# A four-layer image model: where one normalisation runs, and in which order the neighbourhood layer's parts are written

## The chip, the cores and the metric

The kernel runs on one core of one Trainium2 chip. The metric is the device time of one execution in microseconds (us). The engines are TensorE (PE in the profile; PEld is its weight load), VectorE (DVE), ScalarE (ACT), GpSimd (POOL) and SyncE (SP), which issues the transfers. Each engine runs its own instructions in the order in which they were written, and waits where an operand is not there yet or where the place of a result is still in use.

## The reference, cut to what matters

The input is a batch of four images of 56 x 56 pixels with 128 channels. Four layers follow each other. The change touches the first, and one step of the second.

```python
# layer 0: neighbourhood attention (7 x 7 window, 4 heads of 32 channels), then an MLP
xn = layernorm(x);  q, k, v = split(xn @ w_qkv + b_qkv)
x = x + softmax(q . k_window + rpb) @ v_window @ w_proj + b_proj
x = x + gelu(layernorm(x) @ w_fc1 + b_fc1) @ w_fc2 + b_fc2
# layer 1: a gated complex recurrence of 16 steps, per pixel and channel, on g = group_norm(x)
forget = sigmoid(g @ Wf + bf + 2);  let_in = sigmoid(g @ Wi + bi)
delta  = softplus(g @ Wd + bd) * 0.1
h = forget * (A h) + delta * let_in * (B g)          # 16 times; A, B: 2-D Fourier transforms of 7 x 7 kernels
x = x + h
# layer 2: softmax attention over 3136 tokens, and a mixture of 8 experts (2 chosen)
# layer 3: attention by distance, and experts that choose their tokens
```

The sixteen steps are not run one by one. The kernel multiplies them out through powers of the 2 x 2 step, with some 40 elementwise operations for each piece of an image.

## The kernel before, in words

**Stripes and periods.** `neighbourhood_of_safe_scores` works layer 0 off in 28 stripes, seven for each image, of eight pixel rows (four tiles of 112 pixels) each. One turn of its main loop is a period: it writes the 25 parts of the table `PERIOD` once, in the table's order. Every part has a lag: ("scores", 1) in period i works on stripe i+1, ("mlp_out", -2) on stripe i-2. So up to five stripes are under way at a time. The engines TensorE, VectorE and ScalarE take the work in exactly this order (`manual_schedule`); nothing reorders it.

**The parts.** `norm_ahead`, `tokens`, `keys`, `queries` and `values` prepare a stripe. `scores` and `more_scores` form the scores of the first four and the last three blocks of eight columns, and ScalarE takes their exponentials (L663). `bands` and `more_bands` multiply by the relative bias on VectorE (L670). `start_sums`, `sums` and `more_sums` add up on TensorE, `quotient` divides on VectorE. `project` and `add_attention` end the attention. `second_norm` takes the statistics on VectorE (L750) and the roots in nine small operations on GpSimd (L891 to L899). `norm_mlp` then scales the four tiles into `xn` on GpSimd (L582), `mlp_tokens` turns them on TensorE (L207), and `mlp_hidden`, `mlp_out` and `add_mlp` follow. `exp_table` and `gelu_table` run a one-element function (L833), so that ScalarE loads a table early.

**PSUM.** Most results of TensorE pass through one pool of two banks (`ps1`), which are given out in turn: a matmul group waits until the last but one user of the pool has been read. The scores and the MLP's hidden layer share one place of four banks (`s`).

**The recurrence of image 0 within it.** Layer 1 of image 0 runs inside layer 0 of the later images. `Recurrence.plan` lays its steps into the periods: an entry (2, 17, "sums") of `WORK` is written in the second period after the unit's base, ahead of the part at place 17 of `PERIOD`. An image has seven units, and a unit's base lies two periods behind the one before, so that two units overlap. The Fourier transforms of the kernels (`WAVES_AT`) come first, one piece in each of eight periods, and each piece first fetches a table of waves from memory (L1066). `BEGIN` places the group norm between the two. The transforms' small constants are written at (1, 0).

**A unit's places.** All values of a unit lie in one tile, `parts`, and many share a place with a value that is dead by then (L1159 on). Of these the prediction speaks of two: `one_e`, which ScalarE writes in `delta` (L1212), lies where VectorE's `ab` is until `pair` has read it, and `xs`, which ScalarE fills in `turned` (L1218), lies where `pq` is until `result` and `result_sum` have read it.

**The forget gate.** `forget` forms a sigmoid as 0.5 tanh(z/2) + 0.5: two tanh on ScalarE (L1194), and the last step on GpSimd (L1205). It runs in all 28 units, 21 of them in the later layers of images 1 to 3.

Of the kernel before, what the change touches and what calls it, by code (L numbers as in the profile page):

```python
# [9 lines left out]
F32 = mybir.dt.float32  # L10
BF16 = mybir.dt.bfloat16
AF = mybir.ActivationFunctionType
ALU = mybir.AluOpType
# [4 lines left out]
B, H, W, C = 4, 56, 56, 128  # L18
TOK = H * W
P = 2 * W  # L20
NT = TOK // P
GT = 4
# [16 lines left out]
NQ = EC // ET  # L39

PERIOD = (
    ("scores", 1),
    ("more_sums", 0),
    ("norm_ahead", 3),
    ("mlp_tokens", -1),
    ("values", 1),
    ("statistics", 1),
    ("constants", 1),
    ("quotient", 0),
    ("more_scores", 1),  # L50
    ("tokens", 3),
    ("bands", 1),
    ("mlp_out", -2),
    ("project", 0),
    ("add_mlp", -2),
    ("gelu_table", -2),
    ("mlp_hidden", -1),
    ("add_attention", 0),
    ("second_norm", 0),
    ("start_sums", 1),  # L60
    ("keys", 3),
    ("exp_table", 1),
    ("norm_mlp", 0),
    ("sums", 1),
    ("more_bands", 1),
    ("queries", 3),
)

WORK = (
    (1, 12, "softplus"),  # L70
    (3, 24, "statistics"),
    (2, 25, "product_of_sums"),
    (1, 17, "sources"),
    (1, 20, "forget"),
    (3, 0, "pair"),
    (1, 6, "let_in"),
    (1, 14, "softplus_sum"),
    (3, 6, "result"),
    (1, 7, "delta"),
    (1, 11, "logarithm"),  # L80
    (2, 6, "source_gate"),
    (3, 7, "result_sum"),
    (2, 11, "fourths_trace"),
    (3, 17, "turned_back"),
    (3, 20, "added"),
    (2, 1, "source"),
    (2, 7, "fourths"),
    (2, 6, "traces"),
    (1, 12, "turned"),
    (2, 17, "sums"),  # L90
    (3, 2, "steps"),
    (2, 24, "sums_of_fourths"),
)

BEGIN = (
    (0, 14, "tokens"),
    (1, 25, "mean"),
    (2, 24, "normalise"),
    (2, 19, "root"),
    (2, 11, "squares"),  # L100
)

WAVES_AT = (
    (1, 11, "magnitudes"),
    (0, 12, "squared"),
    (1, 25, "scaled"),
    (0, 1, "products"),
)
UNITS = 9
KK = 128  # L110
# [365 lines left out]
def neighbourhood_of_safe_scores(env: Env, f, work):  # L476
# [17 lines left out]
    with ExitStack() as ctx:  # L494
        tc, nc, ins = env.tc, env.nc, env.ins
        cp = ctx.enter_context(tc.tile_pool(name="n_const", bufs=1))
        bp = ctx.enter_context(tc.tile_pool(name="n_big", bufs=1))
        sp = ctx.enter_context(tc.tile_pool(name="n_small", bufs=3))
        wp = ctx.enter_context(tc.tile_pool(name="n_work", bufs=2))
# [4 lines left out]
        bands = []  # L504
# [34 lines left out]
        held = [{} for _ in range(n)]  # L539
        statistics = [{} for _ in range(B)]  # L540

        def tiles_of(i):
            b, s = stripes[i]
            return env.x[b], slice(s * GT, (s + 1) * GT)
# [29 lines left out]
                    ahead(pending[0])  # L574
                    pending[0] += 1

        def normalised(i):
            x, tiles = tiles_of(i)
            rs, off = held[i]["norm"]
            xn = wp.tile([P, GT, C], F32, tag="xn", name="xn")  # L580
            for j in range(GT):
                nc.gpsimd.tensor_scalar(  # L582
                    xn[:, j, :], x[:, tiles.start + j, :], rs[:, j : j + 1],
                    off[:, j : j + 1], ALU.mult, ALU.add,
                )
            return xn

        def first_norm(i):
            held[i]["xn"] = normalised(i)

        def of_stripe(a, i):

# [242 lines left out]
        with tc.manual_schedule(  # L835
            engines={mybir.EngineType.PE, mybir.EngineType.DVE, mybir.EngineType.Activation}
        ):
            rs, off = f["roots"]
            for i in range(2):
                held[i]["norm"] = (a[:, i * GT : (i + 1) * GT] for a in (rs, off))  # L840
                first_norm(i)
            for i in range(2):
                tokens(i)
                if i == 0:
                    constants()
                keys(i)
                queries(i)
            ahead(2)
            parts = {
                "norm_ahead": first_norm,  # L850
                "norm_mlp": first_norm,
                "exp_table": lambda i: table(AF.Exp),
                "mlp_out": mlp_out,
                "add_mlp": add_mlp,
                "scores": lambda i: weights(i, 0),
                "more_sums": lambda i: add_blocks(i, 1),
                "quotient": quotient,
                "values": values,
                "bands": lambda i: banded(i, 0),
                "mlp_tokens": mlp_tokens,  # L860
                "tokens": tokens,
                "more_scores": lambda i: weights(i, 1),
                "keys": keys,
                "queries": queries,
                "constants": lambda i: late_constants() if i == 0 else None,
                "gelu_table": lambda i: table(AF.Gelu),
                "mlp_hidden": mlp_hidden,
                "project": project,
                "add_attention": add_attention,
                "second_norm": second_norm,  # L870
                "more_bands": lambda i: banded(i, 1),
                "start_sums": start_sums,
                "sums": lambda i: add_blocks(i, 0),
                "statistics": lambda i: ahead_to(i + NG + 3),
            }
            for i in range(-1, n + 2):
                for at, (name, lag) in enumerate(PERIOD):
                    run_all(plan.get((i, at), ()))
                    if 0 <= i + lag < n:
                        parts[name](i + lag)  # L880
                run_all(plan.get((i, len(PERIOD)), ()))

# [114 lines left out]
class Recurrence:  # L997
# [10 lines left out]
    def __init__(self, env, ctx, late):  # L1008

        self.env, self.is_late = env, late  # L1010
        nc = env.nc
        cp = ctx.enter_context(env.tc.tile_pool(name="s_const", bufs=1, side="right"))
        self.gates_w = cp.tile([128, 3, C], F32, tag="gates_w", name="gates_w")

        self.gates_b = cp.tile([128, 4, 2], F32, tag="gates_b", name="gates_b")
        self.late = cp.tile([128, 1], F32, tag="late", name="late")

        self.group = cp.tile([128, C], F32, tag="group", name="group")
        self.tiny = cp.tile([128, 1], F32, tag="tiny", name="tiny")
        nc.gpsimd.memset(self.tiny, 1e-8)  # L1020

        self.fa = cp.tile([128, 3, HALF], F32, tag="fa", name="fa")
        self.fb = cp.tile([128, 2, HALF], F32, tag="fb", name="fb")
        self.fa2 = self.fa[:, 2, :]
        self.taps = cp.tile([WAVES, 2, 2, C2], F32, tag="taps", name="taps")
        self.xT = cp.tile([128, TOK], F32, tag="xT", name="xT")

        self.parts = cp.tile([128, 21, UT * P], F32, tag="parts", name="parts")
        self.small = ctx.enter_context(env.tc.tile_pool(name="s_small", bufs=2, side="right"))
# [79 lines left out]
    def steps(self, b, psum):  # L1109


        env, nc, sides = self.env, self.env.nc, self.SIDES
        sp, x, xT = self.small, env.x[b], self.xT
        held = {}
# [43 lines left out]
        def unit(t0):  # L1158
# [42 lines left out]
            def forget():  # L1201

                f = v["forget"]
                gate(0, f, AF.Tanh, 0.5)
                nc.gpsimd.tensor_scalar(f, f, 0.5, 0.5, ALU.mult, ALU.add)  # L1205

            def delta():
                gate(2, v["delta"], AF.Identity)
# [187 lines left out]
    def plan(self, psum, start, statistics, root_of_all):  # L1396


        plan = {}

        def put(i, at, step):
            plan.setdefault((i, at), []).append(step)

        def put_all(table, i, steps):
            for period, at, name in table:
                put(i + period, at, steps[name])

        constants, parts = self.transforms(psum)
        put(1, 0, constants)
        for i, steps in enumerate(parts, 1):  # L1410
            put_all(WAVES_AT, i, dict(zip(("products", "squared", "magnitudes", "scaled"), steps)))
        tokens, mean, squares, root, normalise, units = self.steps(0, psum)
        put_all(BEGIN, start, {
            "tokens": lambda: run_all(tokens), "mean": mean, "squares": lambda: run_all(squares),
            "root": root, "normalise": lambda: run_all(normalise),
        })
        for u, unit in enumerate(units):
            unit["statistics"] = lambda u=u: statistics(tiles_of(u))
            if unit is units[-1]:
                unit["statistics"] = lambda u=u: (statistics(tiles_of(u)), root_of_all())  # L1420
            put_all(WORK, start + 2 + 2 * u, unit)
        return plan
# [1380 lines left out]
def run_all(pieces):  # L2803
    for piece in pieces:
        piece()
# [203 lines left out]
```

## Time and profile before

| what | value |
|---|---|
| median of three runs | 2571.6 us (2569.08 to 2573.55) |
| the profiled execution | 2573.55 us; its span 2571.7 us, 1.9 us lie around it |
| busy: PE, DVE, ACT, POOL | 2415.7, 1845.8, 1502.2, 309.5 us |
| layer 0 with the recurrence of image 0 | from about 18 us to 644 us of the span |
| PE busy and granted clock, 100 to 200 us | 100.0 of 100 us, 1.00 |
| PE busy and granted clock, 300 to 400 us | 87.7 of 100 us, 0.92 |

Times in the profile's rows count from the start of the span. In a row of the timeline the first number is the start and the second the time from the first to the last of the merged instructions; the bracket at the end is how long the engine had stood idle before it, and for whom. A table by stages gives for each stretch its length, and then for PE, PEld, DVE, ACT and POOL the busy time and the number of instructions, the granted TensorE clock (1.00 is full), the share of time in which DMA engines were busy, and GB/s. One place in the loop is easy to find in every period: the matmul at L732, which begins `project`.

### The profile page before, as it was taken

The page shows a single profiled execution, that of the slowest core. Times are in us where ns is not written, and L with a number is a line of the kernel's source. Part 1 is how long each engine was busy: PE and PEld are TensorE (multiplying, and loading weights), DVE is VectorE, ACT ScalarE, POOL GpSimd, SP SyncE. Part 2 cuts the span into 40 slices and gives each one's busy share as a digit, 9 for nine tenths or more (in the row PEclk, how much of TensorE's full clock was granted, in tenths as well). Part 3 has the DMA queues.
Part 4 walks back from the last instruction along what each step waited for, and adds up shares of the span by engine and source line. Part 5 has one row for each costly group of instructions (what it writes and reads, how often), then busy time and mean ns, then how long its engine had stood idle before and what let it go on. Part 6 is the DMA issues. An engine that isn't in the chain of part 4 may idle for free.

```text
span 2571.7 us, 39538 instructions
## 1 busy us (share of the span) xinstructions
PE 2415.7 (94%) x14685; PEld 1304.8 (51%) x14685; DVE 1845.8 (72%) x5062; ACT 1502.2 (58%) x3205; POOL 309.5 (12%) x612
## 2 busy tenths in 40 slices
PE   5999988988999999999999999999999999997795
PEld 3777666666554555545554444444444433442334
DVE  4566787775599786889868777753788666767563
ACT  3888765664666654676432456565545665754680
POOL 5445454433000000000000000000000000000000
PEclk9999998999999999999999999999999998998687
DMA  5000000000000000000000000000000000002266
GB/s 138 15 8 2 2 2 1 2 2 2 9 1 1 1 1 1 1 1 1 12 1 1 1 1 1 1 1 1 1 1 1 1 1 1 1 1 94 87 257 192
DMA packets 39919, 53.97 MB, mean 21 GB/s; under 512 B 4104, under 2 KB 35443, under 8 KB 35620
## 3 DMA queue, kind: packets, MB, share of 16 engines
q1 hardware_dynamic: 39716, 51.34, 6.2%
q8 instruction: 118, 1.93, 0.3%
q14 instruction: 85, 0.70, 0.1%
HBM read 44.78 MB, written 6.42 MB: 20 GB/s over the span
## 4 chain that ended last, share of the span: by engine, by line


## 5 line engine op out<-in xcount | busy, mean ns | idle before, releaser
L2027 ACT ACTIVATE e<-s_ps 128x448 f32<-128x448 f32 x688 | 368.9, 542 | 531.6 <-PE s_ps L2020 527.2
L2020 PE MATMUL s_ps<-zT,xnT 128*128 128x448 f32 (+1 forms) x1400 | 651.2, 555 | 0.6 <-ACT e L2027 0.6
L2103 PE MATMUL o_ps<-e,keep 128*128 128x448 f32 (+1 forms) x1376 | 646.8, 553 | 0.0
L2103 PEld LDWEIGHTS o_ps<-e,keep 128*128 128x128 f32 (+1 forms) x1376 | 241.3, 190 | 214.6 <-issue 213.6
L2020 PEld LDWEIGHTS s_ps<-zT,xnT 128*128 128x128 f32 (+1 forms) x1400 | 240.7, 189 | 213.0 <-issue 192.8
L1830 ACT ACTIVATE d_ps<-d_ps,half 128x448 f32<-128x448 f32 (+1 forms) x384 | 232.2, 606 | 118.0 <-PE d_ps L1818 115.8
L1824 DVE TENSOR_REDUCE found<-d_ps 128x1 f32<-128x448 f32 x316 | 190.7, 618 | 75.0 <-PE d_ps L1818 72.9
L1550 PE MATMUL y_ps<-experts,xnT 128*112 128x512 f32 x448 | 215.5, 603 | 2.0 <-ACT d_ps L1830 1.7
L207 PE MATMUL xT_ps<-ident,xn 112*128 112x112 f32 x672 | 129.9, 289 | 62.0 <-POOL xn L582 41.4
L1555 DVE TENSOR_TENSOR gated<-y_ps,gate 112x512 f32<-112x512 f32 x224 | 151.5, 686 | 37.8 <-PE y_ps L1550 35.4
L207 PEld LDWEIGHTS xT_ps<-ident,xn 112*128 112x128 f32 x672 | 82.3, 146 | 148.1 <-POOL xn L582 54.9
L1560 DVE TENSOR_TENSOR gated<-gated 112x512 f32<-112x512 f32 (+1 forms) x336 | 152.2, 461 | 3.0
L1818 PE MATMUL d_ps<-q_near,k_near 32*128 32x448 bf16 (+1 forms) x700 | 138.2, 373 | 9.8 <-ACT d_ps L1830 4.0
L1550 PEld LDWEIGHTS y_ps<-experts,xnT 128*112 128x112 f32 x448 | 76.2, 178 | 97.6 <-issue 60.4
L1818 PEld LDWEIGHTS <-k_near 32*128 32x128 bf16 (+1 forms) x700 | 33.4, 92 | 168.1 <-issue 155.1
L582 POOL TENSOR_SCALAR xn<-x,rs,off 112x128 f32<-112x128 f32 x216 | 116.5, 552 | 3.2
L766 ACT ACTIVATE h<-h_ps,b_fc 128x448 f32<-128x448 f32 x112 | 61.7, 633 | 79.1 <-PE h_ps L761 79.1
L775 PE MATMUL f_ps<-w_fc,h 128*112 128x128 f32 x896 | 105.2, 276 | 0.9 <-ACT h L766 0.8
L1650 ACT ACTIVATE xn<-x,g_off,g_rs 112x128 f32<-112x128 f32 x224 | 94.1, 484 | 19.3 <-DVE g_off L1640 9.0
L775 PEld LDWEIGHTS f_ps<-w_fc,h 128*112 128x112 f32 x896 | 101.3, 179 | 2.5 <-ACT h L766 2.3
L670 DVE TENSOR_TENSOR e<-e,band 112x1792 f32<-112x1792 f32 (+3 forms) x56 | 99.6, 1780 | 0.0
L663 ACT ACTIVATE e<-s_ps 112x1792 f32<-112x1792 f32 (+3 forms) x56 | 82.6, 1474 | 17.0 <-PE s_ps L654 16.6
(402 smaller groups left out, 3967.6 us busy)
## 6 DMA issues: line engine op xcount, KB each, us to landing
lot<-in_L_ffn_lots SPq DMA_DIRECT2D x32, 1024.0 KB
out_x<-x SPq DMA_DIRECT2D x28, 224.0 KB
x<-in_x SPq DMA_DIRECT2D x3, 1568.0 KB
x<-in_x SPq DMA_DIRECT2D x7, 224.0 KB
parts<-in_waves SPq DMA_DIRECT2D x8, 173.0 KB
out<-found SPq DMA_DIRECT2D x64, 2.0 KB
w_fc<-in_L_conv_w_fc SPq DMA_DIRECT2D x2, 256.0 KB
experts<-in_L_ffn_expert_w SPq DMA_DIRECT2D x1, 512.0 KB
```

The costliest lines, as they stand in the source:

```text
L207: self.nc.tensor.transpose(ps[:, j * P : (j + 1) * P], xn[:, j, :], self.ident[:P, :P])
L582: nc.gpsimd.tensor_scalar(xn[:, j, :], x[:, tiles.start + j, :], rs[:, j : j + 1], off[:, j : j + 1], ALU.mult, ALU.add,)
L775: nc.tensor.matmul(f_ps[:, j, :], h[:, k, j * P : (j + 1) * P], w_fc2[:, k, :], start=(k == 0), stop=(k == 3),)
L1550: nc.tensor.matmul(y_ps, held["xnT"][g][:, j * P : (j + 1) * P], self.experts[:, 4 * i : 4 * i + 4, :], start=True, stop=True,)
L1555: nc.vector.tensor_tensor(gated[:, some, :], y_ps, gate[:, some].unsqueeze(2).to_broadcast([P, 4, C]), ALU.mult,)
L1560: nc.vector.tensor_tensor(gated[:, :n, :], gated[:, :n, :], gated[:, n : 2 * n, :], ALU.add)
L1818: nc.tensor.matmul(d, held["k"][part, 128 * c : 128 * c + n], held["q"][g][part, :], start=True, stop=True,)
L1824: nc.vector.tensor_reduce(self.found[:, self.most : self.most + 1], d, AX.X, ALU.max)
L1830: nc.scalar.activation(d, d, AF.Relu, bias=self.half[:n], accum_out=self.found[:n, self.sums : self.sums + 1],)
L2020: nc.tensor.matmul(s_ps[i * n : (i + 1) * n, :GW], self.xnT[:, at : at + n], zT, start=True, stop=True,)
L2027: nc.scalar.activation(e[:n], s_ps[:n, :GW], AF.Exp)
L2103: nc.tensor.matmul(sums[:, :GW], self.keep[:n, k, :], e[:n], start=(k == 0 and g - 1 not in pairs), stop=last,)
```

## The change

The MLP's norm gets a function of its own, `mlp_norm`, with four ScalarE activations in place of four GpSimd operations. The last step of `forget` becomes a ScalarE activation with a constant tile `half`. The tables `PERIOD`, `WORK`, `BEGIN` and `WAVES_AT` are written anew, and the transforms' constants move from (1, 0) to (0, 0).

```diff
 PERIOD = (
+    ("more_scores", 0), ("start_sums", 0), ("norm_ahead", 3), ("bands", 0),
+    ("mlp_tokens", -2), ("project", -1), ("more_bands", 0), ("add_attention", -1),
+    ("second_norm", -1), ("mlp_hidden", -2), ("sums", 0), ("statistics", 1),
+    ("more_sums", 0), ("tokens", 3), ("quotient", 0), ("values", 1),
+    ("gelu_table", -2), ("scores", 1), ("keys", 3), ("mlp_out", -2),
+    ("norm_mlp", -1), ("queries", 3), ("add_mlp", -2), ("constants", 1), ("exp_table", -2),
-    ("scores", 1), ("more_sums", 0), ("norm_ahead", 3), ("mlp_tokens", -1),
-    ("values", 1), ("statistics", 1), ("constants", 1), ("quotient", 0),
-    ("more_scores", 1), ("tokens", 3), ("bands", 1), ("mlp_out", -2),
-    ("project", 0), ("add_mlp", -2), ("gelu_table", -2), ("mlp_hidden", -1),
-    ("add_attention", 0), ("second_norm", 0), ("start_sums", 1), ("keys", 3),
-    ("exp_table", 1), ("norm_mlp", 0), ("sums", 1), ("more_bands", 1), ("queries", 3),
 )
 WORK = (
+    (2, 22, "fourths_trace"), (2, 8, "source"), (4, 8, "turned_back"), (1, 17, "sources"),
+    (1, 11, "let_in"), (2, 19, "fourths"), (1, 12, "softplus"), (3, 2, "sums"),
+    (2, 10, "forget"), (3, 15, "steps"), (2, 14, "source_gate"), (2, 15, "traces"),
+    (3, 15, "result"), (2, 9, "softplus_sum"), (1, 9, "delta"), (2, 8, "logarithm"),
+    (3, 2, "sums_of_fourths"), (1, 15, "turned"), (4, 14, "statistics"),
+    (3, 15, "result_sum"), (3, 9, "pair"), (4, 10, "added"), (3, 8, "product_of_sums"),
-    (1, 12, "softplus"), (3, 24, "statistics"), (2, 25, "product_of_sums"), (1, 17, "sources"),
-    (1, 20, "forget"), (3, 0, "pair"), (1, 6, "let_in"), (1, 14, "softplus_sum"),
-    (3, 6, "result"), (1, 7, "delta"), (1, 11, "logarithm"), (2, 6, "source_gate"),
-    (3, 7, "result_sum"), (2, 11, "fourths_trace"), (3, 17, "turned_back"), (3, 20, "added"),
-    (2, 1, "source"), (2, 7, "fourths"), (2, 6, "traces"), (1, 12, "turned"),
-    (2, 17, "sums"), (3, 2, "steps"), (2, 24, "sums_of_fourths"),
 )
 BEGIN = (
+    (2, 2, "mean"), (2, 13, "root"), (0, 23, "tokens"), (2, 6, "squares"), (2, 14, "normalise"),
-    (0, 14, "tokens"), (1, 25, "mean"), (2, 24, "normalise"), (2, 19, "root"), (2, 11, "squares"),
 )
 WAVES_AT = (
+    (0, 8, "squared"), (-1, 11, "products"), (1, 5, "magnitudes"), (1, 10, "scaled"),
-    (1, 11, "magnitudes"), (0, 12, "squared"), (1, 25, "scaled"), (0, 1, "products"),
 )
...
+        def mlp_norm(i):
+            rs, off = held[i]["norm"]
+            for j, (out, x) in enumerate(xn_of(i)):
+                nc.scalar.activation(
+                    out, x, AF.Identity, scale=rs[:, j : j + 1], bias=off[:, j : j + 1]
+                )
...
-                "norm_mlp": first_norm,
+                "norm_mlp": mlp_norm,
...
                 gate(0, f, AF.Tanh, 0.5)
-                nc.gpsimd.tensor_scalar(f, f, 0.5, 0.5, ALU.mult, ALU.add)
+                nc.scalar.activation(f, f, AF.Identity, scale=0.5, bias=self.half)
...
-        put(1, 0, constants)
+        put(0, 0, constants)
```

`norm_ahead` keeps its four GpSimd operations.

More of the change, by code (lines that the diff above doesn't have):

```diff
@@ L41 @@
 PERIOD = (
-    ("scores", 1),
[L43 to L47, printed above, removed]
-    ("constants", 1),
[L49 to L63, printed above, removed]
@@ L64 @@
-    ("sums", 1),
-    ("more_bands", 1),
-    ("queries", 3),
+    ("more_scores", 0),
+    ("start_sums", 0),
+    ("norm_ahead", 3),
+    ("bands", 0),
+    ("mlp_tokens", -2),
+    ("project", -1),
+    ("more_bands", 0),
+    ("add_attention", -1),
+    ("second_norm", -1),
+    ("mlp_hidden", -2),
+    ("sums", 0),
+    ("statistics", 1),
+    ("more_sums", 0),
+    ("tokens", 3),
+    ("quotient", 0),
+    ("values", 1),
+    ("gelu_table", -2),
+    ("scores", 1),
+    ("keys", 3),
+    ("mlp_out", -2),
@@ L67 @@
+    ("norm_mlp", -1),
+    ("queries", 3),
+    ("add_mlp", -2),
+    ("constants", 1),
+    ("exp_table", -2),
 )
 WORK = (
-    (1, 12, "softplus"),
[L71 to L92, printed above, removed]
+    (2, 22, "fourths_trace"),
+    (2, 8, "source"),
+    (4, 8, "turned_back"),
+    (1, 17, "sources"),
+    (1, 11, "let_in"),
+    (2, 19, "fourths"),
+    (1, 12, "softplus"),
+    (3, 2, "sums"),
+    (2, 10, "forget"),
+    (3, 15, "steps"),
+    (2, 14, "source_gate"),
+    (2, 15, "traces"),
+    (3, 15, "result"),
@@ L93 @@
+    (2, 9, "softplus_sum"),
+    (1, 9, "delta"),
+    (2, 8, "logarithm"),
+    (3, 2, "sums_of_fourths"),
+    (1, 15, "turned"),
+    (4, 14, "statistics"),
+    (3, 15, "result_sum"),
+    (3, 9, "pair"),
+    (4, 10, "added"),
+    (3, 8, "product_of_sums"),
 )
 BEGIN = (
[L96 to L100, printed above, removed]
+    (2, 2, "mean"),
+    (2, 13, "root"),
+    (0, 23, "tokens"),
+    (2, 6, "squares"),
+    (2, 14, "normalise"),
@@ L101 @@
 )
 WAVES_AT = (
[L104 to L107, printed above, removed]
+    (0, 8, "squared"),
+    (-1, 11, "products"),
+    (1, 5, "magnitudes"),
+    (1, 10, "scaled"),
 )
@@ L575, in ahead_to, with xn_of, first_norm @@
                     pending[0] += 1
-        def normalised(i):
+        def xn_of(i):
             x, tiles = tiles_of(i)
+            held[i]["xn"] = xn = wp.tile([P, GT, C], F32, tag="xn", name="xn")
+            return [(xn[:, j, :], x[:, tiles.start + j, :]) for j in range(GT)]
+        def first_norm(i):
             rs, off = held[i]["norm"]
-            xn = wp.tile([P, GT, C], F32, tag="xn", name="xn")
-            for j in range(GT):
+            for j, (out, x) in enumerate(xn_of(i)):
                 nc.gpsimd.tensor_scalar(
-                    xn[:, j, :], x[:, tiles.start + j, :], rs[:, j : j + 1],
-                    off[:, j : j + 1], ALU.mult, ALU.add,
-                )
-            return xn
-        def first_norm(i):
-            held[i]["xn"] = normalised(i)
+                    out, x, rs[:, j : j + 1], off[:, j : j + 1], ALU.mult, ALU.add
+                )
+        def mlp_norm(i):
+            rs, off = held[i]["norm"]
+            for j, (out, x) in enumerate(xn_of(i)):
+                nc.scalar.activation(
+                    out, x, AF.Identity, scale=rs[:, j : j + 1], bias=off[:, j : j + 1]
+                )
         def of_stripe(a, i):
@@ L1018, in __init__ @@
         self.group = cp.tile([128, C], F32, tag="group", name="group")
+        self.half = cp.tile([128, 1], F32, tag="half", name="half")
+        nc.gpsimd.memset(self.half, 0.5)
         self.tiny = cp.tile([128, 1], F32, tag="tiny", name="tiny")
```

## The prediction

> **What bounds the kernel now.** I first read the page's slices: outside its two ends the kernel keeps TensorE busy at full clock except in one stretch, about 280 to 600 us. Then I cut layer 0 at the matmul of L732, once a period, and had a table by stages made of the pieces.
>
> ```profile
> 108.56:127.28 18.72, 18.72 (x266) 14.48 (x265) 12.06 (x23) 15.93 (x25) 7.50 (x17) 1.00 0.04 12
> ...
> 424.06:452.40 28.34, 22.09 (x265) 16.18 (x264) 23.07 (x42) 13.27 (x22) 11.22 (x17) 0.88 0.00 1
> 452.40:472.04 19.64, 19.64 (x261) 14.42 (x260) 13.20 (x30) 16.62 (x26) 9.54 (x18) 1.00 0.01 3
> ```
>
> Before the recurrence a period is 18.72 us of unbroken TensorE work. With it, long periods (seven, 26.3 to 28.7 us) alternate with short ones (about 19.6). A long one has only 19.1 us of TensorE work (18.72 less 1.48 for the waves, plus two gates of 0.95), so it loses 9.2; VectorE is full in it and the clock falls to 0.88. The timeline of a long period shows how:
>
> ```profile
> 431.64 0.87 DVE L750 BATCH_NORM_STATS2 st<-x 112x6 f32<-112x128 f32 x4
> ...
> 438.38 6.01 POOL L582 TENSOR_SCALAR xn<-x,rs,off 112x128 f32<-112x128 f32 x8
> ...
> 439.58 0.45 PE L207 MATMUL xT_ps<-ident,xn 112*128 112x112 f32 x1 [3.69 <-POOL xn L582]
> ...
> 442.13 0.82 DVE L1317 SCALAR_TENSOR_TENSOR parts<-parts,gates_b 128x224 f32<-128x224 f32 x2
> 442.63 3.19 PE L636 MATMUL v_ps<-w_qkv,xnT 128*88 128x128 f32 x14
> 442.88 0.64 DVE L722 STREAM_TRANSPOSE oT<-d_ps 128x448 f32<-128x448 f32 x1
> ```
>
> The second norm's statistics end at 432.5; roots and scaling on GpSimd take until 444, and `mlp_tokens` holds TensorE. Behind it `values` runs at half speed (3.19 us against 1.69). `quotient` (L722) queues on VectorE behind the recurrence until 442.88. The waits of layer 0 name the first of these, and one more at the start:
>
> ```profile
> PE xT_ps L207 <- POOL xn L582: 35.2, 27, 3.7
> PE f_ps L1073 <- DMA parts<-in_waves: 9.5, 1, 9.5
> ```
>
> In all, TensorE loses 63 us in the long periods (194.9 less six of 19.1 and a last of 17.2) and 7 in the short ones (1.0 each over 18.6): 70 us.
>
> **The norm on ScalarE.** It takes 28 x 4 operations off GpSimd. The same form on ScalarE:
>
> ```profile
> L582 POOL TENSOR_SCALAR xn<-x,rs,off 112x128 f32<-112x128 f32 x216 | 116.5, 552 | 3.2
> ...
> L1650 ACT ACTIVATE xn<-x,g_off,g_rs 112x128 f32<-112x128 f32 x224 | 94.1, 484 | 19.3 <-DVE g_off L1640 9.0
> ```
>
> Busy over count is 0.42 us each, 1.7 a period. In the wave periods ScalarE has 16.4 us (its timeline rows from 108.3 on, added start to start) and gets 18.1 of TensorE's 18.7. It fits, since nothing in its new order waits late; I take 1 us for all of them, 0 to 8. If the cover fails, `queries`, queued behind the norm, comes late, and `project` waits for its PSUM bank. In the new order statistics (place 8) and norm (20) lie far enough apart for the roots (3.1 us undisturbed, 5.7 beside a full VectorE), and `mlp_tokens` follows in the next period: the 3.7 us wait goes. Table loads stay five a pair of periods.
>
> **The forget gate's last step.** One ScalarE operation like L1212 (0.67 us) replaces 0.60 on GpSimd. Seven lie in layer 0 and are in the sums below. Of the 21 later ones I cost nothing: from 700 to 2000 us TensorE is 99 to 100% busy and ScalarE waits for it 527 us at L2027 alone. Without that cover: 14 us; range -2 to 5.
>
> **The start.** The first wave table lands when the images are through:
>
> ```profile
> 42.04 1.05 PE L654 MATMUL s_ps<-q,kT 32*112 32x112 f32 x32
> ...
> 62.96 2.88 PE L1073 MATMUL f_ps<-parts,taps 113*64 113x196 f32 x16 [9.48 <-DMA parts<-in_waves]
> ```
>
> `products` moves from (1, 1) - entry (0, 1) of wave 1 - to (0, 11), but its transfer stays behind the same image transfers in SP's queue. In TensorE's order the first wave matmul now precedes the second scores of stripe 1, `more_sums` 0, `values` 1, `more_scores` 1, `tokens` 3, `project` 0, `start_sums` 1, `keys` 3, `sums` 1, `queries` 3 and the scores of stripe 2: in the row above, the work from 42.04 to 53.5. Their warm durations (0.98, 1.21, 1.63, 0.78, 0.44, 1.10, 0.57, 0.95, 1.59, 0.95, 0.98) sum to 11.2 us. TensorE waits from about 42 instead of 53.5, for the same landing: +11 us, 9 to 13. The constants' transfers, now awaited one period earlier on VectorE (behind them `bands` of stripe 0), are issued before the images and lie under this wait.
>
> **The recurrence's periods.** VectorE's work is now 20 us in an odd period (A) and 18 in an even one (B), in place of 23 and 13. I walk A from VectorE's first step, with start-to-start times of the rows at 425 to 445 us. `sums`, `sums_of_fourths` 3.3; both bands 3.4; `add_attention` 0.6; `product_of_sums` 1.2; statistics 0.8; `pair` 1.5: 10.8, and at 10.4 its last read of `ab`. Only then may ScalarE write `one_e`, in the same place: 0.7, then the Gelu table 1.3, Gelu 2.2, the `let_in` gate 0.8: 15.4. TensorE is through `more_sums` and `tokens` at 11.2 and needs for `values` the bank that `let_in` filled: **a new wait of 4.3 us**. Meanwhile VectorE does `softplus`, `quotient` (2.2), `steps` (1.2), `result` (2.2): 17.3, or 17.7 where it also takes statistics ahead. Only then may ScalarE's `turned` overwrite `pq` with `xs` (1.5), and behind it the copies of `values` are queued: `keys` waits for their bank till 19.5 (or 19.9), then `keys` 0.95, `mlp_out` 3.5, `queries` 0.95: A takes 24.9 to 25.3. B is TensorE's: 18.65 plus 0.5 for `zT` behind a late ScalarE: 19.2.
>
> What does the 4.3 us gap do to the clock? By the row, TensorE restarts slow after 3.69 us idle and after 9.48 (2.88 us for a wave pair that takes 1.5), and is back at speed some 4.5 us on (67.5). Then `values` and the scores in A end at 20.5, 0.6 behind the 19.9 of the other wait. [...] I take the row: 0.6.
>
> So A 25.7 (loss 6.5, six times: 39), B 0.55 six times: 3, the units' two ends 3.5 (in the last odd period `add_mlp` stands behind `result_sum`, and `project` waits for its bank), the wave periods 1: 47 us in place of 70. The last stripe's MLP chain takes as long as before (project to last add 21.9; now some 21).
>
> **Sum.** -70 + 47 + 11 = -12 us. The profiled execution's 2573.55 becomes 2561.5; it stood 2 above the median, so the forecast for a median is 2571.6 - 12 = **2560 us**.
>
> **Rivals.** (1) *Slower: the new wait in A takes the place of the old.* Each A hangs on one ring, VectorE to 17.5, ScalarE's `turned` and copies 2.1, TensorE 4.5, `add_mlp`. [...] For it: VectorE rests some 4 us in A, waiting for `mlp_out` alone, so no step in the ring has cover. Against: its links are measured in rows of equally full VectorE. (2) *The start costs nothing*: the landing at 62.96 moves up, or the work moved behind it is gained later; 2549. Against it, SP issues the waves at 44.97 only after 16 us of image transfers. (3) *The places do not bind* (ScalarE gets to `turned` later than VectorE anyway): A and B at TensorE's 19.1 and 18.65 plus 0.5; 2560 less 6 x 6 = 2524. Against it, ScalarE is free at 12 of A's 17.5. (4) *Nothing*: the gain between 280 and 600 us is eaten by a ScalarE that is late in wave periods and by the later forget steps (8 + 5): 2572.
>
> **How the numbers follow.** 0.2% (5 us) is about what can be told from no change. My case 0.55, rival 1 0.2, rival 2 0.1, rival 3 0.05, rival 4 0.1. My case's own range adds its ends: A's loss 5.5 to 7.5 (+-6), start +-2, wave periods and later steps -3 to +12; 2551 to 2572, of which some 0.1 lies within 0.2% of no change. Faster: 0.45 + 0.1 + 0.05 and a little of rival 4 = 0.62; same 0.16; slower 0.22. The range takes in half of rival 1 and rival 2: 2544 to 2580.
>
> **What would show it.** Right: TensorE's wait for `xn` near 0 in layer 0; its wait for the first waves 20 to 22 us; between L732 marks 25 to 26 and 19 to 20 us in turn, with rows of TensorE waiting for ScalarE at `values` (4 us) and `keys`, and ScalarE's copies at `turned` waiting for VectorE; layer 0 ending near 632 in place of 644. Wrong: odd periods of 28 us or more; a wait for the waves still near 9.5; wave periods above 19.5; or, beyond layer 0, a changed length of 644 to the end.

## The result

| kernel | median | runs | ratio to before, 95% interval |
|---|---|---|---|
| before | 2572.2 us | 4 (2569.1 to 2573.6) | 1 |
| changed | 2549.75 us | 4 (2545.4 to 2553.1) | 0.9913 (0.9896 to 0.9931) |

The change makes the kernel 22.5 us faster. 2560 was forecast; the time lies in the lower part of the range. The profiled execution of the changed kernel took 2545.4 us (span 2543.6), the fastest of its four. In it layer 0 ends (the start of its last `add_mlp`) at 623.7 us instead of 644.0: 20.3 us of the gain are there, where 12 were forecast.

The table by stages of the changed kernel, cut at the same matmul (it is now at L737), with a wave period, a long and a short one:

```profile
124.68:143.20 18.52, 18.52 (x265) 14.57 (x264) 12.08 (x24) 17.33 (x29) 4.57 (x13) 1.00 0.04 11
383.50:408.86 25.36, 20.90 (x265) 16.06 (x264) 20.21 (x36) 17.25 (x32) 7.07 (x16) 0.93 0.01 2
408.86:427.11 18.25, 18.25 (x261) 14.46 (x260) 16.70 (x37) 15.87 (x26) 5.25 (x13) 1.00 0.01 2
```

The long period is 25.4 us instead of 28.3 and the short one 18.25 instead of 19.6. ScalarE has 17.3 us in a wave period, and the period is shorter, not longer. VectorE has 20 and 17 us of work in the two, where it had 23 and 13.

The waits of layer 0 in the changed kernel (total, times, longest):

```profile
ACT parts L1219 <- DVE parts L1310: 25.0, 6, 4.9
PE v_ps L641 <- ACT parts L1201: 22.1, 6, 4.5
...
PE f_ps L1080 <- DMA parts<-in_waves: 17.5, 1, 17.5
ACT parts L1225 <- DVE parts L1318: 9.7, 6, 1.7
```

TensorE's wait for the normed tokens is gone. In its place stand two waits of ScalarE for VectorE, both named in the forecast, of which only the first reaches TensorE: `values` (L641) waits for ScalarE's gate (L1201), which stands behind `one_e` (L1219), which waits for VectorE's `pair` (L1310); and `turned` (L1225) waits for VectorE's `result` (L1318). The wait for the first waves has grown from 9.5 to 17.5 us. The timeline of one long period:

```profile
392.65 0.67 ACT L1219 ACTIVATE parts<-parts,ones 128x448 f32<-128x448 f32 x1 [4.94 <-DVE parts L1310]
393.34 1.28 ACT L771 ACT_TABLE_LOAD   x1
394.64 2.21 ACT L771 ACTIVATE h<-h_ps,b_fc 128x448 f32<-128x448 f32 x4
396.72 0.80 ACT L1201 ACTIVATE parts<-g_ps,gates_b 128x224 f32<-128x224 f32 x2
397.57 2.90 PE L641 MATMUL v_ps<-w_qkv,xnT 128*112 128x128 f32 x14 [4.46 <-ACT parts L1201]
399.48 1.54 ACT L1225 COPY parts<-xT 64x224 f32<-64x224 f32 x4 [1.54 <-DVE parts L1318]
400.40 1.54 PE L659 MATMUL s_ps<-q,kT 32*112 32x112 f32 x32
401.04 0.96 ACT L645 COPY v<-v_ps 112x512 f32<-112x512 f32 x2
401.87 1.02 PE L610 MATMUL k_ps<-xnT,w_qkv 128*128 128x448 f32 x2
402.72 3.66 PE L780 MATMUL f_ps<-w_fc,h 128*112 128x128 f32 x32
```

Read down: `one_e` (0.67 us), the table, Gelu and the gate follow each other on ScalarE; TensorE stands idle for 4.46 us, then `values` and the scores run slowly (2.90 and 1.54 us, where a wave period has 1.69 and 1.05). When the scores end at 401.94, ScalarE's copies of `values`, which stood behind `turned`, end too (402.0), so `keys` does not wait visibly. `keys` and `mlp_out` run at full speed (1.02 and 3.66 us, as in a wave period).

### The profile page after: what moved, and what is told of

Same layout as the page of the kernel before. It is cut to its first block, busy times and chain, and to the rows that moved or that the text cites. A ratio compares the mean times of both kernels' runs of the same rounds, so it can differ in the third digit from the quotient of the medians.

```text
span 2543.6 us, 39482 instructions
## 1 busy us (share of the span) xinstructions
PE 2397.4 (94%) x14685; PEld 1303.8 (51%) x14685; DVE 1842.6 (72%) x5062; ACT 1557.0 (61%) x3347; POOL 176.9 (7%) x473
## 4 chain that ended last, share of the span: by engine, by line
PE 84%; DVE 9%; ACT 4%; SPq 1%; DMA 1%; issue 1%; DVEq 0%; ACTq 0%
PE s_ps L2027 21%; PE o_ps L2110 20%; PE y_ps L1557 7%; PE d_ps L1825 4%; PE f_ps L780 4%; PE xT_ps L207 3%; PE h_ps L766 3%; PE g_ps L1196 2%; PE v_ps L641 2%; PE s_ps L659 2%; PE p_ps L2307 1%; PE o_ps L713 1%; PE l_ps L2266 1%; PE d_ps L719 1%; PE y_ps L2051 1%; PE q_ps L1789 1%
## 5 line engine op out<-in xcount | busy, mean ns | idle before, releaser
L2027 PE MATMUL s_ps<-zT,xnT 128*128 128x448 f32 (+1 forms) x1400 | 649.4, 554 | 0.6 <-ACT e L2034 0.5
L2027 PEld LDWEIGHTS s_ps<-zT,xnT 128*128 128x128 f32 (+1 forms) x1400 | 240.7, 189 | 212.3 <-issue 191.1
L207 PE MATMUL xT_ps<-ident,xn 112*128 112x112 f32 x672 | 118.8, 281 | 25.0 <-ACT xn L1657 16.9
L1657 ACT ACTIVATE xn<-x,g_off,g_rs 112x128 f32<-112x128 f32 x224 | 94.1, 484 | 19.4 <-DVE g_off L1647 9.0
L766 PE MATMUL h_ps<-zT,w_fc 128*128 128x448 f32 x224 | 89.7, 544 | 0.9 <-ACT zT L760 0.9
L790 DVE TENSOR_TENSOR x<-x,f_ps 112x512 f32<-112x512 f32 x28 | 19.3, 688 | 91.7 <-PE f_ps L780 84.8
```

The lines of the kernel that those rows point to most:

```text
L207: self.nc.tensor.transpose(ps[:, j * P : (j + 1) * P], xn[:, j, :], self.ident[:P, :P])
L766: nc.tensor.matmul(h_ps[:, k, :GW], w_fc1[:, k * 128 : (k + 1) * 128], held[i]["zT"], start=True, stop=True,)
L2027: nc.tensor.matmul(s_ps[i * n : (i + 1) * n, :GW], self.xnT[:, at : at + n], zT, start=True, stop=True,)
```

## Experiments

### 1. The two new waits of the long period

In one kernel `one_e` is written later on ScalarE, behind Gelu and the gate; in another `turned` and `sources` are written later in the period, behind the copies that `keys` needs; a third has both. The places in memory stay shared; giving the two values places of their own was not tried.

```diff
 one_e_late, and in both_late: from delta() to softplus(), just ahead of its reader
-                nc.scalar.activation(v["one_e"], e, AF.Identity, bias=env.ones[:, 0:1])
...
+                nc.scalar.activation(one_e, e, AF.Identity, bias=env.ones[:, 0:1])
```

```diff
 turned_late, and in both_late
-    (1, 17, "sources"),
+    (1, 20, "sources"),
...
-    (1, 15, "turned"),
+    (1, 19, "turned"),
```

> The changed kernel, with the one ScalarE step that writes one_e taken out of delta and written just ahead of softplus, behind the Gelu and the let_in gate. Theory (a ring through both shared places sets the long period): TensorE's wait at values (22 us in six periods) goes, since the gate's bank is read 4 us earlier, but keys still waits for the copies behind turned; the wait moves there and the long periods shorten by some 0.3 us each: 2548 us, long periods still 24.5 to 25.3 us. Rival (the wait at values is a cost of its own): long periods of about 21 us, 2524 us in all.

> The changed kernel, with turned moved from place 15 to 19 (behind the copies of values and keys on ScalarE) and sources from 17 to 20. Theory: the wait at values stays (4.4 us a long period, and the slow clock behind it), keys follows at once; long periods 24.5 to 25.5 us, 2548 to 2551 us in all. Rival (turned alone sets the ring): long periods of about 22 us, 2530 us.

> Both of the two steps moved together. Theory: neither shared place holds TensorE any longer, VectorE and TensorE are next (20.5 and 19.1 us in a long period), a pair of periods falls from 43.6 to about 39 us, times six: 2522 us (2515 to 2530), more than the two single moves add up to. Rival (something else holds the long period, such as VectorE's own order): 2545 us.

| kernel | median (runs) | ratio to before | long periods | layer 0 ends |
|---|---|---|---|---|
| changed | 2549.75 us (4) | 0.9913 | 24.9 to 26.7 | 623.7 |
| `one_e` later | 2565.5 (8) | 0.9969 (0.9959 to 0.9980) | 27.0 to 29.1 | 636.3 |
| `turned` later | 2555.9 (4) | 0.9932 (0.9915 to 0.9949) | 23.7 to 26.9 | 628.4 |
| both later | 2520.1 (4) | 0.9808 (0.9789 to 0.9827) | 19.1 to 20.6 | 593.7 |

Neither alone gains anything. `one_e` alone loses 15.8 us (12.6 of them in layer 0), which neither of its theories had. `turned` alone loses 6.1 us (4.7 in layer 0, of which 2.1 stand ahead of the first `project`) and misses its 2548 to 2551 too. Together they gain 29.6 us, nearly the 27.8 expected. The waits of the kernel with `one_e` later, and the timeline of one of its long periods:

```profile
PE k_ps L610 <- ACT v L645: 34.1, 7, 5.9
PEld h_ps L766 <- issue: 33.5, 175, 0.3
ACT parts L1224 <- DVE parts L1318: 32.3, 6, 5.6
```

```profile
397.96 1.89 PE L641 MATMUL v_ps<-w_qkv,xnT 128*112 128x128 f32 x14 [0.43 <-ACT parts L1201]
...
399.77 1.05 PE L659 MATMUL s_ps<-q,kT 32*112 32x112 f32 x32
...
404.44 1.54 ACT L1224 COPY parts<-xT 64x224 f32<-64x224 f32 x4 [5.56 <-DVE parts L1318]
...
406.64 1.86 PE L610 MATMUL k_ps<-xnT,w_qkv 128*128 128x448 f32 x2 [5.81 <-ACT v L645]
...
408.30 4.24 PE L780 MATMUL f_ps<-w_fc,h 128*112 128x128 f32 x32
```

`values` and the scores are now nearly at speed (1.89 and 1.05 us). But VectorE is through `result` no earlier in the period (ScalarE's `turned` starts 16.5 us behind the L737 mark, where it was 16.0), so the idle time now comes at `keys`: 5.8 us in one piece. Now `keys` takes 1.86 us instead of 1.02 and `mlp_out` 4.24 instead of 3.66, and nothing lies beside them that hides this 1.4 us; in the changed kernel the slow work was `values` and the scores, in time that was lost anyway. That accounts for most of the 2 us that a long period grew; the rest of the 15.8 us is not traced here. The two waits hang on one chain, VectorE's, and the second is covered while the first is there. With both gone the clock stays at 1.00 in the long period too:

```profile
374.05:394.63 20.58, 19.44 (x265) 14.61 (x264) 18.91 (x36) 16.61 (x32) 7.09 (x16) 1.00 0.01 2
394.63:413.45 18.82, 18.46 (x261) 14.46 (x260) 17.80 (x37) 16.61 (x26) 5.26 (x13) 1.00 0.01 2
```

### 2. The start

The first two of the eight tables of waves are fetched behind the recurrence's other constants, ahead of images 1 to 3.

```diff
+        for c0 in (0, n):
+            fetch_waves(c0)
...
-            nc.sync.dma_start(waves, ins["waves"]...[:, :, cols])
+            if c0 >= 2 * n:
+                fetch_waves(c0)
```

> The changed kernel with the wave tables of stripes 0 and 1 fetched ahead of the images instead of behind the first wave's set-up. If the 17.5 us in front of the first wave matmul is the late transfer alone, the wait goes, the stripes start that much earlier and the time is 2549.8 less 13 to 18: about 2534. Rival: the transfer only changes places in its queue with the images, the statistics of the first stripe come as much later, and the time is 2547 to 2552.

Measured: 2539.6 us (2538.6 to 2540.5, ratio 0.9872, 0.9855 to 0.9888), 10.1 us less than the changed kernel, and layer 0 ends 8.3 us earlier. Neither theory's number: the wait for the waves goes (17.5 us), but images 1 to 3 come later in the queue, VectorE waits for one of them, and TensorE behind it. From the waits of VectorE up to 75 us, and TensorE's timeline, with the tables fetched early:

```profile
DVE st_all L560 <- DMA x<-in_x: 15.5, 3, 13.7
```

```profile
41.37 0.36 PE L713 MATMUL o_ps<-e,v 88*32 88x88 f32 x8 [3.23 <-DVE e L675]
59.55 0.66 PE L698 MATMUL d_ps<-beside,pad_w 49*128 49x48 f32 x2 [4.91 <-DVE oT L727]
```

The same wait of VectorE for an image was 2.5 us in the changed kernel. So the loss at the start was real: of its 17.5 us 10.1 could be bought back, and about 7 went to the later image.

### 3. Which part of the change carries the gain

The change has three parts: the norm's engine, the forget step's engine, and the written orders. First, each engine move taken back alone from the changed kernel:

```diff
  norm_on_gpsimd                    forget_on_gpsimd
-  "norm_mlp": mlp_norm,            -  nc.scalar.activation(f, f, AF.Identity, scale=0.5, bias=self.half)
+  "norm_mlp": first_norm,          +  nc.gpsimd.tensor_scalar(f, f, 0.5, 0.5, ALU.mult, ALU.add)
```

> The changed kernel, with the MLP's norm back on GpSimd and all orders as changed. Theory (the new order takes the wait for xn away, the engine does not matter): layer 0 as long as in the changed kernel within 3 us, TensorE's waits for xn under 3 us in all, 2550 us. Rival (the engine is what gains): TensorE waits for xn again, 10 us or more, 2560 us or more.

> The changed kernel with the forget gate's last step back on GpSimd. The prediction costs the 28 steps at nothing, -2 to 5: 2545 to 2552. If the 2 us by which the kernel is shorter beyond layer 0 come from this step, the time is 2552.

Then the engine moves made in the kernel before, with its orders untouched (the edits are the same lines the other way round, with `mlp_norm` and `half` added):

> The kernel before with the second norm's last step alone moved to ScalarE, its place in the order unchanged. If the engine carries the gain: about 2556, for 2.3 us less of wait in each of seven long periods. If the order carries it: 2575 to 2600, since the copies of the queries and the first exponentials stand behind a norm that waits for its statistics.

> The kernel before with both engine moves (second norm and the forget gate's last step on ScalarE) and none of the written orders. The norm alone in this order took 19.4 us off. If the forget step is free, this is 2551 to 2556 like the norm alone; since VectorE waits 12 us in layer 0 for the forget step behind GpSimd in that run, up to 6 us less are possible: 2547. If ScalarE is full in this order, 5 us more: 2559. Against the changed kernel's 2549.8 the difference is what the written orders are worth together.

> The kernel before with the forget gate's last step alone moved to ScalarE; norm and orders unchanged. In the profile of before VectorE waits 37.2 us in seven places for this step, 5.3 us a unit, behind the second norm on GpSimd. If these waits hold the ring of the recurrence and so TensorE: 15 to 30 us less, 2543 to 2557. If TensorE is held by the norm anyway: 2568 to 2577, as moving this step on top of the norm cost 3.5 us.

And the two orders mixed: an entry of one kernel's `WORK` is put at the place and period of the other's counting that stands for the same point of a period (in the first, place p becomes p - 17 of the same period, or p + 8 of the one before, and most of `BEGIN` is turned too; in the second the other way round, `WORK` alone). The first is the kernel before with these tables and nothing else: although its text has norm and forget step on ScalarE, both are on GpSimd in it. The second is the changed kernel with `WORK` turned, both on ScalarE.

> The order of the parts of the kernel before with the recurrence's steps in the changed kernel's order and spread over the period (turned into the other order's counting). Norm and forget stay on ScalarE. If the gain lies in the spread of the recurrence's steps, most of it stays: 2550 to 2558. If it lies in the place of the second norm, this is at 2570 or above, with the 2.3 us wait for the normed tokens back in every long period.

> The changed kernel's order of the parts with the recurrence's steps of the kernel before (turned into the other order's counting). If the gain lies in the place of the second norm, the time is 2545 to 2555, and the wait at the values, which comes from the place of the step that lets the input in, goes or moves. If it lies in the spread of the steps: 2565 to 2575.

| norm on | forget on | orders | median (runs) | ratio to before | layer 0 ends |
|---|---|---|---|---|---|
| GpSimd | GpSimd | before | 2572.2 us | 1 | 644.0 |
| ScalarE | GpSimd | before | 2553.5 (4) | 0.9931 (0.9910 to 0.9952) | 625.4 |
| GpSimd | ScalarE | before | 2549.1 (5) | 0.9911 (0.9897 to 0.9924) | 630.0 |
| ScalarE | ScalarE | before | 2557.0 (5) | 0.9940 (0.9926 to 0.9953) | 635.5 |
| GpSimd | ScalarE | new | 2547.4 (4) | 0.9900 (0.9883 to 0.9916) | 624.8 |
| ScalarE | GpSimd | new | 2555.4 (5) | 0.9939 (0.9925 to 0.9952) | 627.5 |
| ScalarE | ScalarE | new | 2549.75 (4) | 0.9913 (0.9896 to 0.9931) | 623.7 |
| GpSimd | GpSimd | old parts, new steps | 2628.4 (4) | 1.0224 (1.0204 to 1.0243) | 698.3 |
| ScalarE | ScalarE | new parts, old steps | 2592.2 (4) | 1.0076 (1.0059 to 1.0093) | 667.1 |

In the whole time one line of the change gives as much as all of it: the forget step alone on ScalarE, 2549.1. The norm alone gives nearly as much, 2553.5. In layer 0 it is the other way round: the profiled executions show 14.0 us less for the forget step, 18.6 for the norm and 20.3 for the change. What the forget step gains beyond layer 0 is taken up in the section on the prediction. What it gains within layer 0 has its reason in the profile of before, in a short period, in rows that the forecast did not use (the first is from the waits of 40 to 640 us):

```profile
DVE parts L1246 <- POOL parts L1205: 37.2, 7, 5.9
...
415.75 3.46 POOL L582 TENSOR_SCALAR xn<-x,rs,off 112x128 f32<-112x128 f32 x8
419.19 0.56 POOL L1205 TENSOR_SCALAR parts<-parts 128x448 f32<-128x448 f32 x1
419.79 0.39 DVE L1246 TENSOR_TENSOR parts<-parts 128x224 f32<-128x224 f32 x1 [5.57 <-POOL parts L1205]
```

The forget step runs on GpSimd behind the norm's roots and eight scaled tiles, and VectorE stands idle for it: 37.2 us in seven units. It is written ahead of those tiles (place 20; `norm_mlp` has 21), but the tables fix the order of three engines, and GpSimd is not one of them. VectorE is not the bound in a short period, so this seems free. It isn't: what VectorE leaves undone moves into the long period, where it is full and where the second norm's statistics stand behind it. The table by stages with the forget step alone moved shows it, and below it what TensorE still waits for in layer 0:

```profile
415.76:441.10 25.34, 22.39 (x266) 16.57 (x265) 18.65 (x35) 13.29 (x22) 11.21 (x17) 0.87 0.00 1
441.10:461.98 20.88, 20.30 (x262) 14.55 (x261) 18.20 (x36) 17.09 (x27) 10.39 (x17) 1.00 0.01 2
...
PE xT_ps L207 <- POOL xn L582: 26.6, 43, 2.3
```

VectorE's 23 and 13 us have become 18.65 and 18.20: the same work, and no step moved in any table. Leaving the step on GpSimd, ahead of the tiles, was not tried; as an estimate it could have ended some 3.5 us of each wait, the tiles' 3.46. The norm still holds TensorE there (26.6 us in 43 waits, none over 2.3; it was 35.2 us in 27, up to 3.7), and the clock in the long period is still 0.87; but a pair of periods is 45.6 us on average instead of 47.6. Moving the norm alone shortens the same queue on GpSimd; in that kernel, up to 640 us:

```profile
DVE parts L1256 <- POOL parts L1215: 12.2, 7, 2.3
PE v_ps L646 <- ACT zT L765: 14.3, 18, 0.8
```

VectorE's wait for the forget step falls from 37.2 to 12.2 us. So each remedy takes away most of the same wait, from one side or the other, which is why they need not add up. With both in the old orders the time is even 7.9 us above that of the forget step alone. There the norm on ScalarE has a price, the second row above: TensorE waits for ScalarE, and in either kernel with it a wave period is 19.5 us instead of 18.7. In the new orders it is 18.5; that is where these earn something. Why both together also end layer 0 10.1 us later than the norm alone, which pays the same price, is not shown.

With the new orders the forget step on GpSimd costs 5.7 us, which lies above the 2545 to 2552 expected. In layer 0 it is 3.8, and the trace shows where: all but one unit lose next to nothing, and one period is 22.9 us instead of 18.25. GpSimd in that period:

```profile
374.90 4.81 POOL L901 TENSOR_TENSOR off<-apart_g,exponent 112x28 f32<-112x28 f32 x1
379.80 0.21 POOL L902 TENSOR_SCALAR rs<-off 112x28 f32<-112x28 f32 x1
380.10 0.25 POOL L904 TENSOR_TENSOR off<-off,sums_g 112x28 f32<-112x28 f32 x1
380.31 0.57 POOL L1212 TENSOR_SCALAR parts<-parts 128x448 f32<-128x448 f32 x1
```

The roots for a whole image (28 columns, 4.81 us) happen to stand ahead of the forget step; VectorE waits 5.14 us for it and TensorE, later, 4.27 us for VectorE.

The mixed orders were worse than both. The first is 55.5 us slower than before, from which it differs in these tables alone; its expectation was made for another kernel, with both steps on ScalarE. The second is 42.4 us slower than the changed kernel and slower than either of its expectations. With the old parts TensorE waits for VectorE's bands (44.6 us in layer 0, 15 times, up to 4.7) and for ScalarE's reading of a gate (16.9 us ahead of `keys`); with the new parts it waits at the recurrence's own matmul for ScalarE's `zT` (27.3 us, 6 times). The counting had to be translated, so these show that the two tables belong to each other, not what either is worth.

### 4. The best version

Both later places of the first experiment and the early tables of the second, in one kernel.

> The two later places (one_e in the place of pair, sources and turned later) and the early wave tables together. The waits lie in different periods, so the gains add: 2520.1 less 10 is 2510. If the early start only moves stripes ahead into a wait that the recurrence sets: 2515 to 2520.

Measured: 2509.45 us (2507.8 to 2511.4), ratio 0.9757 (0.9744 to 0.9770). These gains do add up, as expected: 30 and 10 us, in different places. It is 62.9 us faster than before and 40.3 faster than the change.

## Why the prediction was right or wrong

Direction and range were right; the time was 10 us lower than said. By steps:

- **The norm on ScalarE**: right in price (four tiles in 1.64 us) and nearly so in the wave periods, which it put at 1 us longer in all and which are some 0.2 us shorter each. The wait for `xn` went as said. But in the new orders it is gone with the norm on GpSimd too (2547.4), and in the old ones with the norm on ScalarE (35.2 us in all become 4.3): what was put down to engine and places together needed one of the two. The cover for ScalarE's work that the forecast feared to lose is lost in the old orders, 0.8 us a wave period, and holds in the new.
- **The start, +11 us**: right. TensorE's waits ahead of the first wave matmul are 17.54 and, shortly before, 3.57 us, together the "20 to 22"; in before they were 9.48 and 0.95: 10.7 us more. Rival 2, which had the start free, names 2549 and so comes nearest to the measured time, by luck: its mechanism is refuted.
- **The long period, 25.7 us**: right. The six measure 25.4 on average, with 4.5 us of waiting at `values` as named. Of the second wait, at `keys`, nothing is seen on TensorE: the slow scores end (401.94) when the copies do (402.0). So the slow clock cost nothing visible, where 0.6 was taken. No pause came about ahead of `keys` and `mlp_out`, since the slow work lasted until the copies were done: they took 1.02 and 3.66 us, as in a wave period. In the kernel with `one_e` later a single gap of 5.8 us stood just ahead of these two, and there they took 1.4 us more (1.86 and 4.24). That the new wait costs as much as the old (rival 1, half of which the range takes in, up to 2580) is not shown: the 25.4 us stand against 27.8 on average in before (194.9 over seven).
- **The short period, 19.2 us: mis-sized.** It measured 18.25, but for one of 19.31. Its TensorE work had been put at 18.65, and 0.5 was added for a wait for `zT` that did not occur. Six of these are 4.6 us, the long periods 2.0, the end of the last stripe (19.4 from the last project to the end of layer 0, where "some 21" was said) 1.6: 8.2 of the 8.3 us by which layer 0 ended earlier than the 632 said. That the sum closes is in part luck. The wave periods and the units' two ends are not in it, and on the side of before there is a slip: the six short periods there average 19.48 us, which is 5.3 us of loss over 18.6 and not 7.
- **The forget step, at nothing: the step that failed as a reading.** The forecast looked for its price on ScalarE and found none. It did not ask what the step cost where it was. It saw VectorE full with 23 us beside 13 and took that as given; the run with this step alone moved shows that the 5.6 us of waiting for GpSimd made it so. In the old orders this one line is worth as much as the whole change; in the new ones it measured 5.7 us, of which 3.8 in layer 0. For layer 0 this did not matter, since the walk through the new long period counted VectorE's work in the new order, which does not contain the wait.
- **Rival 3, places that do not bind**, named 2524. They do bind; with both written later the time is 2520.1. So the rival had the price of the two places nearly right: it gave them 36 us (6.5 six times would be 39), and they measured 29.6.
- **Beyond layer 0** the forecast put the gain at nothing, and a changed length there was one of its signs of being wrong. The length did change. By the medians, less what layer 0 shows, some 2 us were gained there, and as much can be put down to the forget step. The first 560 of the 1400 matmuls of L2020 (L2027 in the changed kernel) span a stretch in which 17 of its 21 later steps run, 649 to 1164 us in before. They take 514.2 to 515.2 us in the four kernels with the step on GpSimd and 512.2 to 513.2 in the ten with it on ScalarE; three pairs among these differ in this step alone. So the later steps were not free either; 2 us lie within the -2 to 5 given for them. The rest of what the profiled executions show stays open: from the end of layer 0 on they take 1927.8 us in before and 1919.9 in the changed kernel, but also 1927.0 with `turned` later, whose code is there the same as the changed kernel's. The mean granted clock of this part is 0.96 in before and 0.97 in the changed kernel; that of the whole execution is 0.962, 0.965 and 0.959 in the three.

## What to carry to other kernels

An idle wait on an engine that does not bound its own stage can still be the cause of the next stage's loss. Where the work of one engine is uneven from period to period, ask what it stood idle for in the light one before blaming the full one. Where two waits hang on the same chain, removing one can be worth nothing or less: here each alone made the kernel slower and both together gained 29.6 us. The idle time gathered at the wait that was left, and in front of work that nothing hid it cost 1.4 us of slow matmuls in a long period. And before a change of several parts is credited to its largest part, each part is tried alone in the old kernel: here two different lines gave 19 and 24 us, and both together 15.

## What was not expected of the hardware

- The power in GpSimd's roots takes 1.03 us for 4 columns and 4.81 us for 28 (L901 of the changed kernel, both with 112 partitions), a long block for whatever else is queued there.
- A table of waves (173 KB) moves slowly: while nothing else is under way, from 53 to 62 us of the changed kernel, the queues move 22 GB/s, and the DMA engines are busy 7% of the time, a mean over the 16 that the view counts, which adds up to 1.1 of them; with the images it is 120 to 300 GB/s. Fetched ahead of images 1 to 3, two such tables hold these up: VectorE's wait for an image grew from 2.5 to 15.5 us. Why the tables move so slowly is not shown, and a table of another shape was not tried.
- After a gap of 5.8 us, two matmuls of `keys` took 1.86 us instead of 1.02, and the next 32 of `mlp_out` 4.24 instead of 3.66; after one of 4.46 us, `values` took 2.90 instead of 1.69 and the scores 1.54 instead of 1.05.
